# Output stage of a gated pair kernel: factor and bias of the output gate applied column by column in one scalar-tensor-tensor instead of an eight-column product and a sixteen-column addition

## The chip, the cores and the metric

The kernel runs on one core of one Trainium2 chip. The metric is the device time in microseconds (us) of one execution; the median of three runs is used. The core's engines, as the profile names them, are PE (matrix multiply, with PEld for its weight loads), DVE (the vector engine), ACT (the scalar engine with its activation functions), POOL (GpSimd) and SP (which issues DMA transfers). Each engine works through its own queue of instructions in order and waits on semaphores for the others.

## The reference, cut to what matters

The input x is 512 x 512 positions of 64 channels in float32. Two layers follow each other; the change lies in the first.

```
x = x + L0(_gn(x))                       # group norm of x, then layer 0
x = x + L1(_gn(x))                       # group norm, then a 12 x 12 mode spectral layer

L0:
  xn    = LN(x) * norm_w + norm_b        # over the 64 channels of a position
  left  = (xn @ left_w  + left_b)  * mask * sigmoid(xn @ lgate_w + lgate_b)
  right = (xn @ right_w + right_b) * mask * sigmoid(xn @ rgate_w + rgate_b)
  out_gate = sigmoid(xn @ ogate_w + ogate_b)
  out   = einsum('bkjd,bkid->bijd', left, right)
  out   = LN(out) * onorm_w + onorm_b
  return (out @ out_w + out_b) * out_gate
```

What the change touches is the argument of the last sigmoid, `xn @ ogate_w + ogate_b`. The kernel folds the norm's weight and mean into the matrix (`gate_x`) and the norm's bias into the bias, so that for each position the 64 channels out of the matrix multiply have one number left to be multiplied by, the position's reciprocal standard deviation `rs`, and a row of 64 biases to be added.

## The kernel before

Positions with a zero in the sequence mask need no pair product; the rows that do are compacted first (at most 256 of them, which the inputs here satisfy), and the function `compact` holds all the stages: statistics of x for the group norm, the left and right projections, the 64 pair products, and then the output stage, in which everything around the change lies. After it come the statistics' end, the spectral mixing of 12 x 12 modes, and a last pass over all of x that adds the spectral result and writes the output.

In the output stage x is worked on in 32 units (`units`), each 128 partitions (rows of the image, 2 halves of 128 rows) times 64 columns of 64 channels; a unit has eight steps `n` of eight columns. The order of the instructions on each engine is written out by hand (`tc.manual_schedule()`), in one loop over `s` (L1395). One pass of this loop is one step. For step `s` it puts down, by engine:

- PE: four transposes of the columns that are needed 13 steps later (`t_ps`, L1157, `LEAD` = 13), the four products with `gate_x` of this step (`w_ps`, helper `times`, L1165), and the four products with `center_x` of 12 steps later (`c_ps`, also L1165), from whose squares the variance comes. At steps 0 and 4 of a unit PE also takes the finished unit before through the row basis (`transform`, f_ps, L1320). `w_ps` and `c_ps` have two PSUM buffers each, so PE can be two steps ahead at most of the engine that empties them.
- ACT: the copy of the transposed columns to SBUF (`xt_c`, L1160), on every second step the sigmoid over sixteen columns of a finished `z_t` (L1416), the squares of `c_ps` (`sq_c`, L1188), and once a unit the square root (`rs_n`, L1267).
- POOL: on alternate steps the product of the gate with the output projection (`gated`, L1289) and its addition to x (`added`, L1293), both over sixteen columns, and the indirect DMA loads of later units (L656).
- DVE: four group statistics per step of the unit before (`bn_stats`, `stats2c`, L1348), on every second step the sum of the squares (`summed`, L1261), once a unit the reciprocal (L1458), and the gate's factor and bias: per step a product of eight columns of `w_ps` with the factors (`rs`, from the tile `rs_n`, broadcast over the 64 channels) into half of a `z_t` tile (L1464), and after every odd step one addition of the bias row over the whole `z_t` of sixteen columns, in place (L1466). That bias row is a copy in PSUM, `bias_ps["ogate"]`, part of the tile `scratch`. The original, `rows_of["ogate"]` (tile `bias_row_ogate`, 128 x 64), lies in SBUF. `z_t` comes from a pool of four buffers, which POOL frees with L1293.

So the way of sixteen columns is: PE (`w_ps`) to DVE (L1464 twice, L1466) to ACT (sigmoid, L1416) to POOL (L1289, L1293), and the sum of POOL is then read by DVE (L1348) and PE (L1320) in the next unit. The last two column groups of the last unit leave POOL to DVE (`finished`, L1301 and L1304), after which DVE does the last statistics and the group norm's end.

Of the kernel before, what the change touches and what calls it, by code (L numbers as in the profile page):

```python
# [12 lines left out]
ALU = mybir.AluOpType  # L13
# [4 lines left out]
P = 128  # L18
N = 512
C = 64  # L20
# [26 lines left out]
def conv_preact_kernel(ctx: ExitStack, tc: tile.TileContext, t: dict):  # L47
    nc = tc.nc
# [591 lines left out]
    def compact(fc):  # L640
# [48 lines left out]
        rows_of = {}  # L689
# [7 lines left out]
        with tc.tile_pool(name="wt", bufs=1) as cp:  # L697
# [113 lines left out]
            with tc.tile_pool(name="fn", bufs=3) as np_, tc.tile_pool(name="fw", bufs=2) as wk, tc.tile_pool(  # L811
# [7 lines left out]
                totals, rss, rbs, xns, todo = {}, {}, {}, {}, []  # L819
# [100 lines left out]
                for q in range(-lead - 1, groups):  # L920
# [15 lines left out]
                    if live(lead - QB + early_by) and (q + lead - QB + early_by) % QB == QB - 1:  # L936
                        k = (q + lead - QB + early_by) // QB
# [30 lines left out]
        with held:  # L968
# [66 lines left out]
            with tc.manual_schedule(), tc.tile_pool(name="late", bufs=1) as lp:  # L1035
# [63 lines left out]
                with tc.tile_pool(name="np_x", bufs=LEAD + 2) as tp, tc.tile_pool(name="np_q", bufs=2) as sqp, tc.tile_pool(  # L1099
# [15 lines left out]
                    bias_ps = {"out": scratch[:, 2, :C], "ogate": scratch[:, 2, C:]}  # L1115
# [21 lines left out]
                    xts, rss, sqs, us, zs, fs, st = {}, {}, {}, {}, {}, {}, {}  # L1137
# [24 lines left out]
                    def times(pool, name, s, w):  # L1162
                        ps = pool.tile([P, 8, C], F32, name=name)
                        for i in range(4):
                            nc.tensor.matmul(ps[:, 2 * i : 2 * i + 2, :], xts[s][:, i, :], w, start=True, stop=True)  # L1165
                        return ps
# [228 lines left out]
                    for s in range(first * SIZE, total_g + 2 * SIZE):  # L1395
                        k, n = divmod(s, SIZE)
# [7 lines left out]
                        wps = cps = None  # L1404
                        if s < total_g:
                            wps = times(ps_w, "w_ps", s, gate_x)
# [6 lines left out]
                        if n % 2 == 0:  # L1413
                            i, c = (0, n // 2 - 1) if n >= 2 else (1, 3)
# [11 lines left out]
                        if n % 2 == 1:  # L1426
                            i, c = (0, (n - 3) // 2) if n >= 3 else (1, 3)
# [4 lines left out]
                        else:  # L1432
                            i, c = (0, (n - 4) // 2) if n >= 4 else (1, 2 + n // 2)
# [25 lines left out]
                        if wps is not None:  # L1459
                            c, odd = divmod(n, 2)  # L1460
                            if not odd:
                                z = zp.tile([P, 16, C], F32, name="z_t")
                            rs = rss[k][:, 8 * n : 8 * n + 8].unsqueeze(2).to_broadcast([P, 8, C])
                            nc.vector.tensor_mul(z[:, 8 * odd : 8 * odd + 8, :], wps, rs)  # L1464
                            if odd:
                                nc.vector.tensor_add(z, z, bias_ps["ogate"].unsqueeze(1).to_broadcast([P, 16, C]))  # L1466
                                zs[v, c] = z

                        if n == 7 and held(0) and v < last:
# [16 lines left out]
                        i = s - (first + last - 1) * SIZE - 3  # L1486
# [151 lines left out]
    with tc.If(rows_with_mask < K + 1) as few:  # L1638
        with tc.tile_pool(name="fconst", bufs=1) as fc:
            compact(fc)  # L1640
# [71 lines left out]
```

## Time and profile before

The median of three runs is 1730.91 us (1727.4 to 1731.59). The profiled execution took 1732.75 us, of which the span from the first to the last instruction is 1731.0 us.

| | whole span (1731.0 us) | output stage, one unit (1009.54 to 1030.51 us) |
|---|---|---|
| PE busy | 1552.3 us, 90% | 20.85 of 20.97 us |
| DVE busy | 1402.3 us, 81% | 20.76 of 20.97 us |
| ACT busy | 950.2 us, 55% | 16.08 of 20.97 us |
| POOL busy | 933.0 us, 54% | 20.40 of 20.97 us |
| granted PE clock | 0.898 | 1.00 |
| DMA engines' share | | 0.53 |

The first L1464 starts at 700.06 us and the last L1466 at 1400.29 us; that is the output stage. The pass over all of x that follows, from about 1430 us to the end, keeps the DMA engines busy all the time (a share of 1.01 between 1450 and 1600 us) at a granted PE clock of 0.50. "Busy" is the time in which at least one instruction of the engine was running; the instructions of one engine may overlap, so that the mean duration times the count can be more than the busy time. For DVE the distance from start to start is therefore as important as a duration. The timeline view merges neighbours of one kind into one row: its "us" is then from the first start to the last end, and "x4" says how many there were.

### The profile page before, as it was taken

The numbers are of one execution on the slowest core, as the hardware profiler recorded it, in microseconds if no ns is written. First come the engines' busy times: TensorE is split into PE (matmuls) and PEld (weight loads), VectorE is DVE, ScalarE is ACT, GpSimd is POOL, SyncE is SP. The second block draws the span as 40 slices with busy tenths as digits, with TensorE's granted clock in tenths as the row PEclk, the third lists the DMA queues.
The fourth block names the chain that finished last, engine by engine and source line by source line (L and its number), as shares of the span: only waits on it lengthen the run. The fifth ranks groups of instructions, "written<-read, shape, count | busy, mean of one in ns | idle before, by whom it ended". The sixth has DMA issues, their size and how long they took to land. (4 is left out here: it accounts for less than half of the span.)

```text
span 1731.0 us, 32443 instructions
## 1 busy us (share of the span) xinstructions
PE 1552.3 (90%) x10928; PEld 1235.1 (71%) x10928; DVE 1402.3 (81%) x2978; ACT 950.2 (55%) x1748; POOL 933.0 (54%) x695
## 2 busy tenths in 40 slices
PE   6898899998999988989999999999999868998772
PEld 6766766655999877878888988898889635665431
DVE  7999788886555589889999999999999975774541
ACT  3666677764333488667777777777777632001000
POOL 4666111110000068989999999999999871111110
PEclk9999999999999999999999999999999975555555
DMA  7999278878999788577777767777777699999998
GB/s 288 420 419 419 85 237 295 287 254 282 305 306 304 246 296 339 203 246 259 249 250 263 248 240 252 266 244 246 252 264 249 202 347 414 426 426 427 426 427 375
DMA packets 187024, 518.46 MB, mean 300 GB/s; under 512 B 36160, under 2 KB 102976, under 8 KB 141920
## 3 DMA queue, kind: packets, MB, share of 16 engines
q1 hardware_dynamic: 152560, 295.71, 47.3%
q0 software_dynamic: 30816, 218.38, 34.2%
q10 hardware_dynamic: 3472, 2.20, 0.5%
q8 instruction: 89, 1.46, 0.3%
q14 instruction: 87, 0.71, 0.1%
HBM read 311.60 MB, written 204.60 MB: 298 GB/s over the span
## 5 line engine op out<-in xcount | busy, mean ns | idle before, releaser
L1165 PE MATMUL w_ps<-gate_x,xt_c 128*128 128x128 f32 x2016 | 277.1, 281 | 31.7 <-DVE z_t L1464 26.1
L1293 POOL TENSOR_TENSOR xc<-xc,z_t 128x1024 f32<-128x1024 f32 x127 | 300.9, 2370 | 8.0
L1165 PEld LDWEIGHTS w_ps<-gate_x,xt_c 128*128 128x128 f32 x2016 | 249.2, 195 | 47.7 <-DVE z_t L1464 43.4
L1165 PE MATMUL c_ps<-center_x,xt_c 128*128 128x128 f32 x1952 | 264.8, 279 | 0.0
L1165 PEld LDWEIGHTS c_ps<-center_x,xt_c 128*128 128x128 f32 x1952 | 242.1, 195 | 2.0 <-ACT xt_c L1160 1.1
L1618 PE MATMUL l_ps<-xc,rinv 24*128 24x512 f32 x512 | 207.8, 1126 | 29.7 <-DVE xc L1625 19.4
L1348 DVE BATCH_NORM_STATS2 stats2c<-xc 128x6 f32<-128x128 f32 x1024 | 220.7, 280 | 8.2 <-POOL xc L1293 8.2
L1416 ACT ACTIVATE z_t<-z_t 128x1024 f32<-128x1024 f32 x128 | 135.5, 1058 | 133.5 <-DVE z_t L1466 124.4
L1618 PEld LDWEIGHTS l_ps<-xc,rinv 24*128 24x128 f32 x512 | 120.6, 304 | 112.1 <-DVE xc L1625 58.1
L1247 POOL TENSOR_TENSOR xc<-xc,bias_row_out 128x1024 f32<-128x1024 f32 x32 | 75.2, 2359 | 232.2 <-PE y_ps L1176 213.8
L1160 ACT ACTIVATE xt_c<-t_ps,ab_xc 128x512 f32<-128x512 f32 x252 | 173.0, 687 | 20.7 <-PE t_ps L1157 20.6
L1464 DVE TENSOR_TENSOR z_t<-w_ps,rs_n 128x512 f32<-128x512 f32 x256 | 172.4, 674 | 11.9 <-PE w_ps L1165 11.8
L1466 DVE TENSOR_TENSOR z_t<-z_t,scratch 128x1024 f32<-128x1024 f32 x128 | 156.3, 1221 | 9.8 <-ACT rs_n L1267 3.4
L1188 ACT ACTIVATE sq_c<-c_ps 128x512 f32<-128x512 f32 x244 | 143.3, 588 | 32.7 <-PE c_ps L1165 32.1
L1289 POOL TENSOR_TENSOR z_t<-z_t,xc 128x1024 f32<-128x1024 f32 x64 | 151.6, 2369 | 15.0 <-ACT z_t L1416 14.9
L1157 PE MATMUL t_ps<-c_ident,xc 128*128 128x128 f32 x1024 | 158.8, 278 | 0.0
L787 DVE BATCH_NORM_STATS2 stats1c<-x_ps 128x6 f32<-128x512 f32 x256 | 154.3, 684 | 4.9 <-PE x_ps L786 3.0
L1157 PEld LDWEIGHTS t_ps<-c_ident,xc 128*128 128x128 f32 x1024 | 118.3, 142 | 52.2 <-issue 51.0
L1625 DVE TENSOR_TENSOR xc<-xc,l_ps 128x512 f32<-128x512 f32 x176 | 109.5, 683 | 55.5 <-DMA xc<-x_h,dst_i 44.5
L1289 POOL TENSOR_TENSOR z_t<-z_t,bias_row_out 128x1024 f32<-128x1024 f32 x63 | 149.7, 2377 | 3.3 <-ACT z_t L1416 2.8
L1261 DVE TENSOR_REDUCE scratch<-sq_c 128x16 f32<-128x1024 f32 x122 | 148.0, 1213 | 1.5
L761 ACT COPY xc<-xg 128x128 f32 x352 | 105.0, 298 | 48.3 <-DMA xg<-in_x,src_i 28.0
(250 smaller groups left out, 2643.6 us busy)
## 6 DMA issues: line engine op xcount, KB each, us to landing
x_h<-xc SPq DMA_DIRECT2D x64, 1024.0 KB
out_x<-xc SPq DMA_DIRECT2D x44, 1024.0 KB
sides_d<-o_c SPq DMA_DIRECT2D x64, 512.0 KB
xc<-u_d SPq DMA_DIRECT2D x512, 64.0 KB
out_x<-lx_t SPq DMA_DIRECT2D x20, 1024.0 KB
left_raw<-sides_d SPq DMA_DIRECT2D x64, 256.0 KB
right_raw<-sides_d SPq DMA_DIRECT2D x64, 256.0 KB
tri_d<-tri_t SPq DMA_DIRECT2D x64, 256.0 KB
```

Source lines behind the costliest of these rows:

```text
L787: nc.vector.bn_stats(stats[:, 0, 16 * (jc % quarter) + 4 * r + c, :], ps.rearrange("p i k -> p (i k)"))
L1157: nc.tensor.transpose(tps[:, i, :], flat[:, o : o + P], ident)
L1160: nc.scalar.activation(xts[s], tps, AF.Identity, bias=ab1[:, 2:3])
L1165: nc.tensor.matmul(ps[:, 2 * i : 2 * i + 2, :], xts[s][:, i, :], w, start=True, stop=True)
L1188: nc.scalar.activation(sqs[s // 2][:, 8 * (n % 2) : 8 * (n % 2) + 8, :], cps, AF.Square)
L1261: nc.vector.tensor_reduce(totals[k % 2][:, 8 * (n - 1) : 8 * (n + 1)], sqs.pop(s // 2), AX.X, ALU.add)
L1289: nc.gpsimd.tensor_mul(zs[k, c], zs[k, c], u)
L1293: nc.gpsimd.tensor_add(xr, xr, zs.pop((k, c)))
L1348: nc.vector.bn_stats(st[k // 4][:, g, k % 4, :], x_of(k)[:, :, 2 * g : 2 * g + 2])
L1464: nc.vector.tensor_mul(z[:, 8 * odd : 8 * odd + 8, :], wps, rs)
L1466: nc.vector.tensor_add(z, z, bias_ps["ogate"].unsqueeze(1).to_broadcast([P, 16, C]))
L1618: nc.tensor.matmul(ps.rearrange("p j o -> p (j o)"), rinv[h, b, :], it[h], start=True, stop=True, tile_position=(32 * g, 0),)
```

## The change

For each step, the one product of 128 x 512 elements becomes eight instructions of 128 x 64 elements, one for each column. Each is a scalar-tensor-tensor: the column's 64 channels in PSUM, times the column's factor (a scalar for each partition, read through a pointer from `rs_n` in SBUF), plus the bias row in SBUF. The addition L1466 is dropped, and nothing in the stage reads the PSUM copy of the gate's bias any more. Over the stage 256 products and 128 additions become 2048 scalar-tensor-tensors. The other engines' instructions keep their number and order. Of the eight of a step the first has the waits (for PE's `w_ps`, and for POOL where a new `z_t` buffer begins); the other seven have none.

```diff
                             c, odd = divmod(n, 2)
                             if not odd:
                                 z = zp.tile([P, 16, C], F32, name="z_t")
-                            rs = rss[k][:, 8 * n : 8 * n + 8].unsqueeze(2).to_broadcast([P, 8, C])
-                            nc.vector.tensor_mul(z[:, 8 * odd : 8 * odd + 8, :], wps, rs)
+                            for i in range(8):
+                                nc.vector.scalar_tensor_tensor(
+                                    z[:, 8 * odd + i, :], wps[:, i, :], rss[k][:, 8 * n + i : 8 * n + i + 1],
+                                    rows_of["ogate"], ALU.mult, ALU.add,
+                                )
                             if odd:
-                                nc.vector.tensor_add(z, z, bias_ps["ogate"].unsqueeze(1).to_broadcast([P, 16, C]))
                                 zs[v, c] = z
```

## The prediction

> **What bounds the kernel now.** I first read the busy time by stage, to see which engine is full where the change lies. One unit of the output stage, from one reciprocal (L1458) to the next:
>
> ```profile
> core 0: us, PE busy (x) PEld busy (x) DVE busy (x) ACT busy (x) POOL busy (x), PEclk, DMA share, GB/s
> 1009.54:1030.51 20.97, 20.85 (x180) 18.45 (x180) 20.76 (x50) 16.08 (x25) 20.40 (x11) 1.00 0.53 185
> ```
>
> Three engines are nearly full: PE, DVE and POOL. Busy time alone doesn't say which of them sets the pace, so the waits of the stage come next (microseconds in total, times, longest), here from 900 to 1350 us:
>
> ```profile
> ACT z_t L1416 <- DVE z_t L1466: 75.0, 53, 2.6
> ...
> PEld w_ps L1165 <- DVE z_t L1464: 19.4, 31, 2.2
> ...
> DVE z_t L1464 <- PE w_ps L1165: 3.4, 4, 1.5
> ```
>
> ACT and PE wait for DVE's z_t far more than DVE waits for PE. DVE is the pacer, with PE and POOL just behind it. All waits of DVE over the whole stage, 700 to 1403 us:
>
> ```profile
> DVE z_t L1464 <- PE w_ps L1165: 11.8, 8, 5.3
> DVE stats2c L1348 <- POOL xc L1293: 8.2, 5, 2.8
> DVE z_t L1466 <- ACT rs_n L1267: 3.4, 7, 0.9
> DVE c_ps L1301 <- ACT z_t L1416: 0.4, 1, 0.4
> ```
>
> That is 23.8 us of some 703. In the rest DVE goes from one instruction to the next, so what it is given in addition lengthens the stage, apart from what fits into these 23.8 us. After the stage nothing is changed, and the pass that follows starts when DVE has finished; a later end of the stage moves it as a whole.
>
> **The cost of what is removed.** Durations overlap on DVE, so I take distances from start to start. Two steps in the middle of the stage:
>
> ```profile
> 1018.82 0.68 DVE L1464 TENSOR_TENSOR z_t<-w_ps,rs_n 128x512 f32<-128x512 f32 x1
> 1019.42 0.86 DVE L1348 BATCH_NORM_STATS2 stats2c<-xc 128x6 f32<-128x128 f32 x4
> 1020.20 0.67 DVE L1464 TENSOR_TENSOR z_t<-w_ps,rs_n 128x512 f32<-128x512 f32 x1
> 1020.90 1.22 DVE L1466 TENSOR_TENSOR z_t<-z_t,scratch 128x1024 f32<-128x1024 f32 x1
> 1022.04 0.87 DVE L1348 BATCH_NORM_STATS2 stats2c<-xc 128x6 f32<-128x128 f32 x4
> ```
>
> The even product occupies 1019.42 - 1018.82 = 0.60 us. The odd one occupies 0.70 us, since the addition behind it waits until it has ended (0.66 to 0.78 in other pairs, mean 0.71). The addition occupies 1022.04 - 1020.90 = 1.14 us. A pair of steps pays 0.60 + 0.71 + 1.14 = 2.45 us, and 128 pairs 313 us.
>
> **The cost of what is added.** 16 scalar-tensor-tensors for a pair, each 64 elements long, with a pointer scalar, one operand in PSUM and one in SBUF. The trace has this form at 256 elements (L1010), a cousin at 512 (L951), and short ones with a pointer scalar but one tensor (L133, L119):
>
> ```profile
> 529.77 0.88 DVE L1010 SCALAR_TENSOR_TENSOR tri_t<-tri_c_ps,mask_own,mask_s 128x256 f32<-128x256 f32 x2 [1.13 <-PE tri_c_ps L1005]
> ```
>
> ```profile
> 330.39 1.41 DVE L951 SCALAR_TENSOR_TENSOR o_c<-sides_c,b_all,sigc 128x512 f32<-128x512 f32 x2 [1.25 <-ACT sqc L859]
> ```
>
> ```profile
> 11.22 0.23 DVE L133 TENSOR_SCALAR src_i<-c_iota,base 128x16 int32<-128x16 f32 x1
> 11.36 0.87 DVE L119 TENSOR_SCALAR hot<-c_iota,rank_p 128x128 f32<-128x128 f32 x4
> ```
>
> Two of L1010 take 0.88 us and one 480 ns, so the second starts 0.40 us after the first. For L951 it is 1.41 - 0.746 = 0.664 us. 256 elements more cost 0.264 us, 1.03 ns each; the start-to-start distance is thus about 0.136 us and then 1.03 ns an element. Down to 64 elements that gives 0.40 - 192 x 1.03 ns = 0.202 us. A line from L133 (16 elements, the next one starts 0.14 to 0.15 us later) to L1010 gives 0.145 + 48 x 1.06 ns = 0.196 us. I take 0.198 us. L1010 is the nearest row by far, as its operands lie in the same memories. The rows put bounds around it. Below: the statistics without a pointer scalar (L1348), 128 elements, start every (0.87 - 0.28) / 3 = 0.197 us, and L119 with one likewise; less 64 elements that is 0.130 us. Above: if the short instructions didn't overlap, each would take its whole duration, 480 - 192 x 1.03 = 282 ns.
>
> 2048 x 0.198 = 406 us in place of 313: **DVE gets 92 us more**, 2.9 us a unit, of which a part falls into its present waits.
>
> The Trainium skill speaks against the change at this point. "VectorE: DVE Perf Modes", section "The TRN2 errata", states a fixed latency for each instruction, 120 cycles at 0.96 GHz beside one cycle an element where PSUM is read, and advises tiles of at least 512 elements so that it is paid seldom. By this rule a product would cost 0.66 us, the addition 1.19 and a scalar-tensor-tensor of 64 elements 0.19, so a pair would go from 2.51 to 3.07 us, and the stage would gain 72 us before any wait is filled. The rows' fixed part for this form, 0.136 us, is near that figure, but they also show 0.065 us for instructions without the pointer scalar, which the rule doesn't separate.
>
> **What of it falls into waits.** I went through DVE's waits in order of time. In the first 11 steps (700.06 to 726.85 us) DVE has no statistics yet and PE sets the pace. Waits of 1.34, 0.58, 0.87 and 1.15 us stand there, 3.9 in all; the 11 x 0.36 us that the change adds there fit in. The wait for POOL at 726.85 (2.64 us) stays, since POOL begins no earlier. From 748 to 798 us POOL is behind (0.31, 5.31, 2.12 and 0.28 us, the long one through PE, whose L1320 waits for POOL's L1293). POOL needs 20.40 us a unit, and a unit of DVE will take 20.97 + 2.9 = 23.9, so POOL catches up: 8.0 us. Four later waits for PE's w_ps (0.63, 1.04, 0.19, 1.53) go likewise, as PE has 20.85 us of work a unit: 3.4 us. Six waits of L1466 put down to ACT (0.28 to 0.55, 2.5 in all) go with L1466, which alone read the PSUM copy. At 1390.80 DVE waits 2.81 us for POOL near the end, where POOL will be ahead. Sum 20.6 us. If none of it went the change would cost 92 us; more than 23.8 can't go.
>
> **The other engines.** PE, ACT and POOL keep their instructions and get 2.9 us of slack a unit. The sigmoid waits for the end of a pair on DVE as before; POOL and the next unit's statistics are queued behind it, and their slack covers it. w_ps is held for about 1.6 us (8 x 0.198) in place of 0.68, and PE must refill it: its next w_ps products (8 x 0.28 us for two steps) fit into the 6 us of two DVE steps. If this cover were gone, DVE would wait at its first instruction of a step, 1 us at most by the difference of the two holds.
>
> **Sum.** 92 - 20.6 = +72 us. The profiled execution (1732.75 us, span 1731.0) lies 1.8 us over the median of the runs, 1730.91; on the median the change makes **1803 us**.
>
> **Rivals.**
> *A, the pointer scalar costs nothing more when instructions follow densely.* Place: the start-to-start distance on DVE. For it: L119, eight in a row, 0.197 us for 128 elements with a pointer scalar, no more than L1348 without one. Against it: L1010 and L951, with the same operands as here, 0.136 us fixed. At 0.130 us a pair costs 2.08 us in place of 2.45 and DVE loses 47 us; but PE (20.85 of 20.97) and POOL (20.40) then bound the stage, and 0.12 to 0.57 us a unit is left to be won, 4 to 18 us over 32 units: about 1722 us. The change is not slower from 2.45 / 16 = 0.153 us an instruction downward.
> The Trainium skill has a reason why L119 may not be a witness: "VectorE: DVE Perf Modes", section "The perf-mode tier table", lets a float32 tensor_scalar in SBUF take two elements a cycle, so that L119's 128 would stream like 64; by that L119 itself gives 0.197 us for our instruction. No row tells its streaming rate apart from its fixed part.
> *B, no overlap between the short ones.* For it: a dependent pair does not overlap (L1464 to L1466). Against it: the eight of a step are independent, and L1010's two overlap. 2048 x 0.282 = 578 us, +265 - 21: 1975 us.
> *C, the PE clock falls.* A slower stage leaves PE busy about 20.85 / 23.9 = 87%. Between 1400 and 1450 us, with PE busy 68%, the granted clock is 0.65. PE would become the bound below a clock of 20.85 / 23.9 = 0.87; at 0.75 a unit would take 27.8 us, 32 x 3.9 = 125 us more: about 1928 us. Against it: between 0 and 100 us PE is busy 80% and from 600 to 700 us 86%, both at 1.00.
> *D, the waits stay.* PE or POOL waits return elsewhere and nothing of the 20.6 us is filled: 1823 us. The same cause on DVE, so it belongs to the range.
>
> **Chances and range.** The forecast with D and the rounding of the timeline (0.195 to 0.205 us an instruction, -6 to +14 us): 0.84. A: 0.06. B: 0.05. C: 0.05. The range, 1785 to 1830 us, takes the forecast from -18 (0.195 us: -6, all waits filled: -3, and 9 us for what I have not seen, some 0.3 us a unit) to +27 (0.201 us: +6, nothing filled: +21) and leaves A, B and C out. A measurement of this kernel can tell about 0.3% (5 us) from no change. A splits into faster 0.04 and same 0.02; all else is slower, 0.94.
>
> **What would show it.** In the profile after: L1464 as SCALAR_TENSOR_TENSOR 128x64, 2048 times, each near 270 ns, eight of them merged in about 7 x 0.198 + 0.27 = 1.66 us; L1466 gone; a unit of 23.9 us between reciprocals with DVE busy throughout and PE and POOL at 85 to 88%; DVE's waits under 8 us in all; the pass after the stage as long as before. A distance under 0.153 us, or a unit that PE or POOL fills, would make the forecast wrong.

## The result and the profile after

The changed kernel takes 1796.64 us (median of 4 runs, 1793.02 to 1797.93) where the kernel before takes 1731.25 us in the same comparison: a ratio of 1.0367, 95% interval 1.0342 to 1.0393, or 65 us more. The forecast was 72 us more.

The page after, the row of the new instructions (columns: line, engine, operation, tiles and shapes, count, then busy time and mean ns of one, then the idle time before them and what ended it):

```profile
L1464 DVE SCALAR_TENSOR_TENSOR z_t<-w_ps,rs_n,bias_row_ogate 128x64 f32<-128x64 f32 x2048 | 410.1, 272 | 3.7 <-PE w_ps L1165 3.5
```

It stands first on the page with 410 us. Before, L1464 and L1466 together were busy for 172.4 + 156.3 = 329 us. The timeline of the changed kernel in the stage, two steps:

```profile
1038.37 1.62 DVE L1464 SCALAR_TENSOR_TENSOR z_t<-w_ps,rs_n,bias_row_ogate 128x64 f32<-128x64 f32 x8
1039.90 0.86 DVE L1348 BATCH_NORM_STATS2 stats2c<-xc 128x6 f32<-128x128 f32 x4
1040.68 1.61 DVE L1464 SCALAR_TENSOR_TENSOR z_t<-w_ps,rs_n,bias_row_ogate 128x64 f32<-128x64 f32 x8
1042.20 0.86 DVE L1348 BATCH_NORM_STATS2 stats2c<-xc 128x6 f32<-128x128 f32 x4
1042.98 1.21 DVE L1261 TENSOR_REDUCE scratch<-sq_c 128x16 f32<-128x1024 f32 x1
```

Eight of them occupy DVE for 1039.90 - 1038.37 = 1.53 us; over the stage's 241 groups of eight without a wait the mean is 1.519 us, 0.190 us for each. A pair of steps now costs 3.04 us in place of 2.45. The reader sees two different numbers for one instruction: 272 ns from its start to its end, 190 ns from its start to the next one's. Only the second adds up to the stage. The busy time of stretches (first the kernel before, then the changed one, both from 1000 to 1300 us; the columns are length, then busy time and count of PE, PEld, DVE, ACT and POOL, the granted clock, the DMA engines' share, GB/s):

```profile
1000.00:1300.00 300.00, 291.13 (x2459) 256.23 (x2459) 295.00 (x697) 223.78 (x331) 285.14 (x138) 0.99 0.72 253
```

```profile
1000.00:1300.00 300.00, 269.29 (x2227) 234.07 (x2226) 298.86 (x1280) 204.59 (x302) 260.43 (x126) 0.98 0.66 227
```

Before, PE, DVE and POOL are all at 95% or more; after, DVE alone has no idle time left. PE falls to 90% and POOL to 87%, at a granted clock of 0.98 against 0.99. DVE's waits in the changed kernel, from 690 to 1475 us:

```profile
DVE stats2c L1348 <- POOL xc L1293: 8.2, 3, 4.7
DVE z_t L1464 <- PE w_ps L1165: 3.5, 5, 1.8
DVE f_ps L1237 <- ACT rs_p L1224: 1.0, 1, 1.0
DVE scratch L1261 <- ACT sq_c L1188: 0.4, 1, 0.4
DVE c_ps L1301 <- ACT z_t L1416: 0.4, 1, 0.4
```

Without the one of 1.0 us, which lies ahead of the stage, these are 12.5 us; before there were 23.8. So DVE's work grew by 128 x (3.04 - 2.45) = 76 us, of which 11 us fell into waits: by this sum 65 us. Measured from the first L1464 to L1301, the stage went from 702.6 us (700.06 to 1402.69) to 765.8 us (703.07 to 1468.89), 63.2 us more, so the sum is right to 2 us. The rest of the difference of the two profiles lies outside the stage: it began 3.0 us later, before any changed instruction had run (in the other runs with nothing changed ahead of the stage it began between 699.5 and 706.6 us), and what follows it took 328.3 us before and 327.2 after.

One wait of the second list is new in its size. Near the end of the stage ACT stands in four DMA issues (L1342, small writes to the row spectrum; the profile calls the engine's issuing side ACTq), 7.00 us in the changed kernel and 2.40 before. The kernel before, with DVE's wait for POOL that follows:

```profile
1376.30 2.40 ACTq L1342 DMA_DIRECT2D modes_d<-xc  x4
...
1390.80 0.87 DVE L1348 BATCH_NORM_STATS2 stats2c<-xc 128x6 f32<-128x128 f32 x4 [2.81 <-POOL xc L1293]
```

ACT's timeline in the changed kernel:

```profile
1436.42 0.58 ACT L1328 COPY xc<-f_ps 128x512 f32<-128x512 f32 x1
1437.03 7.00 ACTq L1342 DMA_DIRECT2D modes_d<-xc  x4
1444.11 1.28 ACT L1416 ACT_TABLE_LOAD   x1 [7.11 <-DMA xc<-in_w_real]
1445.40 2.00 ACT L1416 ACTIVATE z_t<-z_t 128x1024 f32<-128x1024 f32 x2
```

Two sigmoids had piled up behind the issues. POOL, which waits for them, and DVE, which waits for POOL's sum, in the same kernel:

```profile
1446.54 2.35 POOL L1289 TENSOR_TENSOR z_t<-z_t,xc 128x1024 f32<-128x1024 f32 x1 [6.70 <-ACT z_t L1416]
```

```profile
1456.10 0.87 DVE L1348 BATCH_NORM_STATS2 stats2c<-xc 128x6 f32<-128x128 f32 x4 [4.73 <-POOL xc L1293]
```

### The profile page after: what moved, and what is told of

It reads as the page before. It is cut to its first block, busy times and chain, and to the rows that moved or that the text cites. A ratio compares the mean times of both kernels' runs of the same rounds, so it can differ in the third digit from the quotient of the medians.

```text
span 1796.1 us, 34317 instructions
## 1 busy us (share of the span) xinstructions
PE 1577.7 (88%) x10928; PEld 1247.5 (69%) x10928; DVE 1482.9 (83%) x4642; ACT 952.9 (53%) x1748; POOL 933.5 (52%) x695
## 5 line engine op out<-in xcount | busy, mean ns | idle before, releaser
L1464 DVE SCALAR_TENSOR_TENSOR z_t<-w_ps,rs_n,bias_row_ogate 128x64 f32<-128x64 f32 x2048 | 410.1, 272 | 3.7 <-PE w_ps L1165 3.5
L1165 PE MATMUL w_ps<-gate_x,xt_c 128*128 128x128 f32 x2016 | 286.2, 287 | 77.0 <-DVE z_t L1464 76.5
L656 POOL DMA_INDIRECT xc<-x_h,dst_i x44 | 41.4, 941 | 158.2 <-DVE xc L1627 91.8
```

What stands on the lines that cost most here:

```text
L1464: nc.vector.scalar_tensor_tensor(z[:, 8 * odd + i, :], wps[:, i, :], rss[k][:, 8 * n + i : 8 * n + i + 1], rows_of["ogate"], ALU.mult, ALU ...
```

## The experiments

Theory: DVE sets the stage's pace, and each instruction with a pointer scalar pays about 0.06 us more from start to start than one without. Rivals: short instructions from PSUM with a second tensor are slow by themselves, pointer or not; or part of the loss comes once, from the stage's end. The times of each run are compared with runs of the kernel before on the same chip (medians 1731 to 1733 us).

**The price of each form, alone.** Into the kernel before, ahead of the stage, nine rows of eight independent instructions were put:

```diff
+        for i in range(8):
+            vec.scalar_tensor_tensor(fo[:, i, :C], fp[:, i % 4, :C], fs[:, i : i + 1], fr[:, :C], mul, add)
+        for i in range(8):
+            vec.scalar_tensor_tensor(fo[:, i, :C], fp[:, i % 4, :C], 0.5, fr[:, :C], mul, add)
+        for i in range(8):
+            vec.tensor_add(fo[:, i, :C], fp[:, i % 4, :C], fr[:, :C])
...
```

`fp` lies in PSUM, `fi`, `fr` and the scalars `fs` in SBUF. Expected:

> The kernel before, with nine rows of eight independent DVE instructions each put ahead of the stage, so that the start-to-start distance of each form can be read alone. Theory (a pointer scalar costs about 65 ns more from start to start, whatever the other operands are): 64 elements with a pointer scalar 0.19 us whether the tensors lie in PSUM or SBUF and whether there are one or two of them (a one-tensor form in SBUF may be less), 0.26 us at 128 elements with PSUM; with an immediate scalar or none 0.13 us at 64. Rival (short instructions with PSUM or with two tensors are slow by themselves, pointer or not): the immediate forms and the plain addition take 0.19 us too. L119's 0.197 us at 128 elements in SBUF: if its elements stream two at a time, the immediate form at 128 takes about 0.13 us and the pointer form at 64 about 0.16; if one at a time, the immediate form at 128 takes 0.20 us.

The timeline of this run (form_ps is in PSUM, form_in and form_row in SBUF; a row with form_scalar has the pointer):

```profile
19.72 1.63 DVE L162 SCALAR_TENSOR_TENSOR form_out<-form_ps,form_scalar,form_row 128x64 f32<-128x64 f32 x8
21.26 1.13 DVE L164 SCALAR_TENSOR_TENSOR form_out<-form_ps,form_row 128x64 f32<-128x64 f32 x8
22.31 1.13 DVE L166 TENSOR_TENSOR form_out<-form_ps,form_row 128x64 f32<-128x64 f32 x8
23.36 1.65 DVE L168 SCALAR_TENSOR_TENSOR form_out<-form_in,form_scalar,form_row 128x64 f32<-128x64 f32 x8
24.93 1.39 DVE L170 TENSOR_SCALAR form_out<-form_in,form_scalar 128x64 f32<-128x64 f32 x8
26.23 1.65 DVE L172 TENSOR_SCALAR form_out<-form_in,form_scalar 128x128 f32<-128x128 f32 x8
27.80 1.17 DVE L174 TENSOR_SCALAR form_out<-form_in 128x128 f32<-128x128 f32 x8
28.88 1.62 DVE L176 TENSOR_SCALAR form_out<-form_ps,form_scalar 128x64 f32<-128x64 f32 x8
30.42 2.15 DVE L178 SCALAR_TENSOR_TENSOR form_out<-form_ps,form_scalar,form_row 128x128 f32<-128x128 f32 x8
```

The distance is the time of the eight less the mean duration of one (0.276, 0.215, 0.215, 0.278, 0.248, 0.278, 0.218, 0.273 and 0.340 us, in this order), by 7: 0.193, 0.131, 0.131, 0.196, 0.163, 0.196, 0.136, 0.192, 0.259 us. (The run took 1745.91 us, 13 us over the kernel before, which is what these rows take.) The pointer costs 0.193 - 0.131 = 0.062 us where the first tensor is in PSUM (L162 less L164) and 0.060 us in the one-tensor form in SBUF (L172 less L174); with the first tensor in SBUF the pointer form takes the same (L168), and the second tensor costs nothing (L176 against L162). 64 elements more cost 0.066 us where PSUM is read (L178 less L162). In the one-tensor form in SBUF they cost 0.033 us (L172 less L170): two elements stream in the time of one, so L119's 0.197 us at 128 elements was the price of 64 with the pointer, and no evidence for a free pointer.

**The pointer taken away.** The norm's factor is replaced by a constant:

```diff
-                                    z[:, 8 * odd + i, :], wps[:, i, :], rss[k][:, 8 * n + i : 8 * n + i + 1],
+                                    z[:, 8 * odd + i, :], wps[:, i, :], 0.5,
                                     rows_of["ogate"], ALU.mult, ALU.add,
```

> The changed kernel with the constant 0.5 in place of the pointer to the factor (the norm's factor is left out of the gate); number and shape of the instructions are the same. Theory (the pointer is what makes them slow): 0.13 us from start to start, a pair of steps 2.08 us on DVE in place of 3.06, DVE falls below PE and POOL, time 1718 to 1731 us. Rival (64 elements from PSUM with a second tensor are slow by themselves): 0.19 us and 1797 us as with the change.

1720.14 us (1718.16 to 1721.81), a ratio of 0.9924 (0.9908 to 0.9941) to the kernel before: the same 2048 short instructions without the pointer are 76 us faster than with it, and even faster than before. Its page's row:

```profile
L1464 DVE SCALAR_TENSOR_TENSOR z_t<-w_ps,bias_row_ogate 128x64 f32<-128x64 f32 x2048 | 287.6, 213 | 12.0 <-PE w_ps L1165 11.9
```

Eight occupy 1.04 us on average, 0.130 us each, and DVE now waits for PE and POOL. One of these waits, 10.3 us for POOL, stands at the stage's end, where ACT was held 9.25 us in L1342's issues, so that the time holds more than the price of the instructions.

**The second tensor taken away.** A product alone, with the pointer; the bias is left out:

```diff
-                                nc.vector.scalar_tensor_tensor(
+                                nc.vector.tensor_scalar(
                                     z[:, 8 * odd + i, :], wps[:, i, :], rss[k][:, 8 * n + i : 8 * n + i + 1],
-                                    rows_of["ogate"], ALU.mult, ALU.add,
+                                    None, ALU.mult,
                                 )
```

> The changed kernel with a product by the pointer scalar alone (tensor-scalar, the gate's bias is left out): the second tensor is taken away and the pointer kept. Theory (the pointer): 0.19 us from start to start, 1790 to 1800 us. Rival (the second tensor, from SBUF beside PSUM, is what costs): about 0.13 us and 1718 to 1731 us.

1796.10 us, ratio 1.0366 (1.0345 to 1.0387), as with the change. The bias addition inside the instruction is free; the pointer is what is paid for.

**Half of the change.** Scalar-tensor-tensors in odd units, products and additions in even ones:

```diff
+                            if v % 2 == 0:
+                                rs = rss[k][:, 8 * n : 8 * n + 8].unsqueeze(2).to_broadcast([P, 8, C])
+                                nc.vector.tensor_mul(z[:, 8 * odd : 8 * odd + 8, :], wps, rs)
-                            for i in range(8):
+                            for i in range(8 if v % 2 else 0):
...
+                                if v % 2 == 0:
+                                    nc.vector.tensor_add(z, z, bias_ps["ogate"].unsqueeze(1).to_broadcast([P, 16, C]))
```

> The change in every second unit only, 16 of 32. Theory (DVE sets the pace in every unit, so the loss is a sum over units): 64 pairs x 0.61 us = 39 us, of which some 6 to 11 us fall into waits: 1759 to 1764 us on a chip where before takes 1731. Rival (a good part of the loss comes once, from the stage's end, where ACT's DMA issue and POOL hold DVE for 4.7 us, or from a filled slack that is used up): more than 1770 us, or under 1750 us.

1765.69 us, ratio 1.0186 (1.0169 to 1.0203): 33 us over the 1732.5 us of before in this comparison, half of the 65. The theory's 1759 to 1764 us were for a before of 1731 us; for 1732.5 they end at 1765.5, so the run lies just at their upper edge, and well under the rival's 1770. DVE's late wait for POOL was 5.94 us here (2.81 before), so about 3 us do come once. The bulk is a sum over units.

**The floor under DVE.** The kernel before without L1466, so without the bias:

```diff
-                                nc.vector.tensor_add(z, z, bias_ps["ogate"].unsqueeze(1).to_broadcast([P, 16, C]))
```

> The kernel before without the addition of the bias row (the gate's bias is left out): DVE is relieved of 4 x 1.14 us and of the addition's wait (4 x 0.11 us) a unit, 20.97 to about 16.0 us. It shows the floor that PE and POOL set. Theory (PE with 20.85 us and POOL with 20.40 us of work a unit are right behind DVE): 1713 to 1731 us, and PE or POOL without idle time in the stage. Rival (PE's and POOL's busy times hold waits for DVE, so that DVE's work is worth its full time in both directions): DVE's 5 us a unit come off, 160 us less, 1570 us.

1718.33 us, ratio 0.9909 (0.9886 to 0.9932). 160 us were taken off DVE and 15 came off the time; DVE then waits (same columns as above):

```profile
DVE stats2c L1348 <- POOL xc L1293: 108.8, 32, 5.2
DVE z_t L1464 <- PE w_ps L1165: 30.7, 30, 7.3
```

From 1000 to 1300 us PE was busy 292.94 us, POOL 292.09 and DVE 236.53: PE and POOL are right behind. Which of the two sets the floor was not separated. So work added to DVE costs almost its full time (65 of 76 us), and of the 160 us removed from it 15 were gained.

**ACT's stall at the stage's end.** The changed kernel with L1342 issued by SP:

```diff
-                            queue = nc.scalar if jc == NJ - 2 else nc.sync
+                            queue = nc.sync
```

> The changed kernel with the four small writes of the second-last row spectrum (L1342) issued by SP in place of ACT. In the changed kernel ACT stood 7.0 us in these issues, the sigmoid behind them came late, POOL idled 6.7 us and DVE waited 4.7 us for POOL. Theory (that wait is on the path): ACT's stall and DVE's wait at this place go, 2 to 5 us less than the change, 1792 to 1795 us. Rival (the wait only moves: SP's queue holds the stores and loads behind it, or POOL is late there anyway): within 1.5 us of the change.

1788.20 us, ratio 1.0322 (1.0299 to 1.0344). A second time, for the size:

> The changed kernel with L1342 issued by SP, a second time, for its size: it gave 1788.2 us where the changed kernel had 1796.6, 8.4 us less, while the two waits that should go with it were worth 4.7 us. If the size holds: 1786 to 1790 us. If the first reading took in the scatter of the runs: 1791 to 1794 us.

1790.09 us, ratio 1.0343 (1.0316 to 1.0370). Where the 4.73 us stood, both profiles show 0.18 us; here the first:

```profile
1451.83 0.87 DVE L1348 BATCH_NORM_STATS2 stats2c<-xc 128x6 f32<-128x128 f32 x4 [0.18 <-POOL xc L1293]
```

So the wait was real and hung on ACT's issues. The gain was 4 to 8 us by the ratios, whose intervals overlap each other and that of the change; the wait at this place accounts for 4.5 us, and the two profiles show where the rest lies. The stage took 758.8 and 758.6 us in them, 765.8 with the change and 763.0 in the run without the second tensor, which has the same late wait (4.47 us): beyond the wait nothing clear of the scatter is gained in the stage. What follows the stage took 324.2 and 324.1 us, against 327.2 and 328.0. Why these 3 us are gained there is not shown.

**A version that is faster than both.** The odd step's product of the kernel before, put ahead of that step's statistics, so that the addition finds it finished:

```diff
+                        c, odd = divmod(n, 2)
+                        if wps is not None and odd:
+                            rs = rss[k][:, 8 * n : 8 * n + 8].unsqueeze(2).to_broadcast([P, 8, C])
+                            nc.vector.tensor_mul(z[:, 8:16, :], wps, rs)
                         if n >= 3 and held(1):
                             statistics(v - 1, range(4 * (n - 3), 4 * (n - 2)))
```

> The kernel before with the odd step's product ahead of that step's four statistics, so that the addition behind them doesn't wait for the product to end (0.71 us of the odd product's slot becomes 0.60). Theory (DVE sets the pace, but PE with 20.85 of 20.97 us is right behind): 128 x 0.11 = 14 us off DVE, of which PE leaves 4 us or so: 1723 to 1729 us. Rival A (DVE's time counts in full): 1717 us. Rival B (the product now waits for PE's w_ps, and the statistics behind it, so the wait only changes its name): 1729 to 1735 us.

1718.50 us (1718.11 to 1722.48), ratio 0.9922 (0.9904 to 0.9939), 14 us less, more than the theory's 2 to 8 and the size of rival A. The timeline (L1467 is the even product, L1449 the odd one, L1469 the addition):

```profile
1024.50 0.69 DVE L1467 TENSOR_TENSOR z_t<-w_ps,rs_n 128x512 f32<-128x512 f32 x1
1025.10 0.69 DVE L1449 TENSOR_TENSOR z_t<-w_ps,rs_n 128x512 f32<-128x512 f32 x1
1025.69 0.87 DVE L1348 BATCH_NORM_STATS2 stats2c<-xc 128x6 f32<-128x128 f32 x4
1026.47 0.55 DVE L1462 RECIPROCAL rs_n<-rs_n 128x64 f32<-128x64 f32 x1
1026.92 1.18 DVE L1469 TENSOR_TENSOR z_t<-z_t,scratch 128x1024 f32<-128x1024 f32 x1
```

The odd product now occupies 0.59 us, and the dependency's 0.11 us lies behind the statistics. The time is that of the run without L1466 (1718.33 us), so relieving DVE further gains nothing in the whole. That floor does not lie in the stage alone: without L1466 the stage was shorter still, 680.0 us against 687.7 here, but what follows it took 333.3 us against 329.0; why is not shown. The theory had taken PE's 20.85 us a unit for its need, and that failed: the unit that begins at 1026.47 took 20.50 us here. What PE's other 0.35 us were, the profile doesn't say. With the queue of L1342 changed as well:

> The kernel before with both edits: the odd step's product ahead of the statistics, and the four small writes of L1342 issued by SP. Theory (the late wait of DVE for POOL, 2.21 us in the run with the product first, comes from ACT's stall in these issues there too): 2 us less than with the product first alone, about 1716.5 us. Rival (at this end of the stage POOL is late in any case, since DVE has less to do in the last steps than POOL): 1717.5 to 1720 us, no difference.

1719.28 us, ratio 0.9924 (0.9904 to 0.9944): no difference. DVE's late wait for POOL stayed, 1.98 us in place of 2.21; in this version it doesn't come from ACT's issues.

## Why the prediction was right

**DVE as the bound** held. Half of the change cost half, and a relief of 160 us on DVE brought 15.

**The price of an instruction** was right in kind and 4% too high. It was put at 0.198 us, from L1010 by 1.03 ns an element; the stage shows 0.190 and the rows of forms 0.193. The fixed part is 0.127 us (0.193 less 64 x 1.03 ns) and not 0.136, and the rounding of the timeline to 0.01 us is not the reason, since the records have 0.401 us between two of L1010. L1010 comes in pairs, and 63 of its 64 pairs begin after a wait. In the first row of the forms, which follows a short pause, the first distance is 0.201 us and the next six are 0.191 to 0.192. Less these 9 ns the sum from L1010 gives 0.194 us. This fits, but it was not tried by itself, and the one pair without a wait has 0.401 us too. Over 2048 instructions the difference is 16 us: 76 in place of 92. The Trainium skill's advice against small tiles ("VectorE: DVE Perf Modes", section "The TRN2 errata") pointed the right way, and its 72 us came near the 76, but its split was not the chip's: the runs show a fixed 0.065 us without the pointer (0.131 less 64 x 1.03 ns) and 0.127 with it, whether the first tensor lies in PSUM or in SBUF. The two elements a cycle of the same page's section "The perf-mode tier table" are there in this case: 0.033 us for 64 elements in the one-tensor SBUF form against 0.066 in the two-tensor form that reads PSUM.

**The waits that it fills** were overrated: 20.6 us forecast, 11.3 filled. The change cost nothing in the first 11 steps, as forecast: 26.79 us before the first statistics and 26.76 after (703.07 to 729.83). But it was not the waits named that were filled. Of their 3.9 us 3.1 stayed, while the wait for POOL at the end of these steps, which was to stay, fell from 2.64 to 0.35 us (first before, then after):

```profile
726.85 0.87 DVE L1348 BATCH_NORM_STATS2 stats2c<-xc 128x6 f32<-128x128 f32 x4 [2.64 <-POOL xc L1293]
```

```profile
729.83 0.88 DVE L1348 BATCH_NORM_STATS2 stats2c<-xc 128x6 f32<-128x128 f32 x4 [0.35 <-POOL xc L1293]
```

POOL's sum came no earlier, counted from the start of the stage, and DVE reached it later. L1466's waits went with it (2.5 us). Of the 8.0 us of waits for POOL between 748 and 798 us one of 3.08 us stayed, and of the 3.4 us of later waits for PE 0.8 stayed. The largest miss is "near the end, where POOL will be ahead": the wait there grew from 2.81 to 4.73 us, because ACT stood in its DMA issues, a queue that the prediction didn't look at. Moving these issues took the wait away.

The two errors, 16 us too much and 9 us too little, have opposite signs, and the sum came out 7 us high; the range held the time. That the forecast came so near is thus in part luck, and the 3.0 us by which the stage began later, for which the prediction had no term, are in the 65 us too.

**The rivals.** A fell in its reason: the pointer costs 0.062 us in dense rows too, and L119 was no witness. Its floor of 1722 us was nearly right (1718 to 1720 us in four runs). B fell: the eight overlap, 272 ns long and 190 apart. C fell: the granted clock is 0.98 in the stage (0.99 before). D is half true, with 11 of 20.6 us. Of the signs named, the duration near 270 ns, the eight in 1.66 us (1.61), the unit of 23.9 us (23.33 from 1034.57 to 1057.90) and the unchanged pass behind were there; waits "under 8 us" were not (12.5), and PE "at 85 to 88%" was not (90% from 1000 to 1300 us).

## What to carry to other kernels

Price short instructions by the distance from start to start of a row of the same form, pointer scalar included, and not by their duration or by the number of elements: here one fused pass over the data in 64-element pieces lost to two passes in 512- and 1024-element pieces, with half the elements to stream. Where an engine is the bound and two others are right behind it, work added to it cost nearly in full here, and work removed was worth only the gap to the next (15 of 160 us here); measure that floor before a larger rewrite. The same gap was won by moving one independent group of instructions between a producer and its consumer on the engine.

## What was not expected of the hardware

- A scalar-tensor-tensor with an immediate costs the same as a plain addition of the same size (0.131 us at 64 elements), and reading the scalar through a pointer adds 0.062 us to each.
- The same four DMA issues took ACT 2.40 us in one kernel and 7.00 us in the other, and nothing else on ACT ran meanwhile; in the changed kernel SP had just issued eight weight loads (1429.5 to 1435.7 us), in the kernel before two (1369.8 to 1371.7 us), with the next at 1380.67 us, after ACT's issues. The other profiles fit: of the eight runs in which ACT issues these four, they took 1.95 to 3.22 us in the four that had one or two such loads in the 9 us before, and 6.74 to 9.25 us in the four that had seven or eight. That these loads are what ACT waited for was not tried by itself.
